# Conv loads begun under the stage before them: shared pools, weights by planes, first images of the last stage in memory early

## The chip, the core and the metric

The kernel runs on one core of a Trainium2 chip. The metric is device microseconds for one execution. The kernel before takes 2425.87 us, the median of 3 runs (2424.24 to 2426.80). The profile is of one further execution, which took 2423.68 us; its recorded span is 2421.5 us.

## What is computed

The input x has 8 images of 256 channels and 56 x 56 pixels, in float32. Two layers follow each other, both of the form "x plus f(group norm of x)".

```python
def _L0_conv_ref(x, w_reduce, b_reduce, w_span, b_span):
    ker = einsum('bchw,oc->bohw', x, w_reduce) + b_reduce
    ker = einsum('bchw,oc->bohw', ker, w_span) + b_span
    ker = ker.reshape(B, G, 1, K * K, H, W)
    ...
    out = (ker * patches).sum(axis=3)

def _L1_conv_ref(x, w1, w2, g1, b1, g2, b2):
    out1 = noised_tri_conv(x, w1)
    out1 = batch_norm_train(out1, g1, b1)
    out1 = jax.nn.relu(out1)
    out2 = noised_tri_conv(out1, w2)
    out2 = batch_norm_train(out2, g2, b2)
    return jax.nn.relu(out1 + out2)

x = x + _L0_conv_ref(_gn(x), ...)
x = x + _L1_conv_ref(_gn(x), ...)
```

The first layer is an involution: each pixel has its own 7 x 7 filter for each of 16 groups. The second layer has two 3 x 3 convolutions with weights quantized to -1, 0 and 1 (the centre tap counts twice). Batch norm needs the mean and variance of a whole convolution's output before the next step may start, so the layer is cut into stages that can't be merged.

## The kernel before, in words

There are four stages, and what one leaves for the next lies in DRAM: x1 (after the involution), y1 (after convolution 1), y2 (after convolution 2).

**Involution** (lines 435 to 864). The 8 images are worked in 32 quarters of 64 channels. Inside a quarter, ten rows of tiles follow each other. For each row TensorE multiplies the filter matrices `a` with input tiles `q` (`apply_row`, L704), ScalarE and VectorE pick the result out of PSUM (L716, L717), and GpSimd adds it to x (L720). Filters of the next quarter are made meanwhile (L671, L675, L680). A hand-written order is pinned on every engine. At the end of a quarter x1 is stored (L732), and after the last quarter one call of `group_norm_params` (L858) makes the scale and shift of the second group norm for all 8 images.

**Convolutions** (`conv_phase`, L242, called once for each). A pass n takes half an image (28 output rows); there are 16 passes. It loads two `raw` tiles (L264), normalizes them on ScalarE into the padded tile `xp` (L870 in convolution 1, L880 with ReLU in convolution 2), and VectorE makes six row-transformed planes of them (`transform`). Each plane is kept as a high part (ScalarE, L294) and a low part (VectorE, L295), whose sum is the float32 value. TensorE then does 6 planes x 2 output halves x 12 matmuls = 144 matmuls of 128 x 392 (L388), in the order of `ORDER`. VectorE combines the planes to rows of y (L374 and L399 to L410), SyncE stores y (L420), and ScalarE sums y and its square for the batch norm (`statistics`, L351), one pass late. The weights are one tile of 4608 KB, loaded at the stage's start (L249). Every pool of the stage is opened at its start and given back at its end.

**Batch norm parameters** (`batch_norm_params`, L163) are a chain of small instructions, mostly on VectorE.

**Last stage** (L887 to L900). For 16 half-channel images it loads y1, y2 and x1 (1568 KB each), does ReLU, multiply-add, ReLU and an add, and stores the result. y1 and y2 have two buffers each, x1 three.

Loads and stores from SyncE go through one queue in program order: an instruction that waits holds up all behind it. The order on each engine is made when the program is built, by a scheduler with priorities.

Of the kernel before, what the change touches and what calls it, by code (L numbers as in the profile page):

```python
# [13 lines left out]
DRAM = bass.MemoryType.DRAM  # L14

P = 128
# [62 lines left out]
def involution_tri_block_kernel(  # L79
# [33 lines left out]
    st1, st2 = (const_tile([P, CT, 2, 2 * B], name) for name in ("st1", "st2"))  # L113
# [128 lines left out]
    def conv_phase(stack, i, src_d, norm, stats, shift, dst_d):  # L242
# [4 lines left out]
        wqp = stack.enter_context(tc.tile_pool(name=f"wq{i}p", bufs=1))  # L247
        wq = wqp.tile([P, WT, CT, 3, C], F32R, tag="wq", name=f"wq_{i}")
        nc.sync.dma_start(wq.rearrange("p w t k o -> p (w t k o)").bitcast(F32), wq_d[i - 1])  # L249
        pad = stack.enter_context(tc.tile_pool(name=f"pad{i}", bufs=1))  # L250
        planes = stack.enter_context(tc.tile_pool(name=f"planes{i}", bufs=8))
        wk = stack.enter_context(tc.tile_pool(name=f"wk{i}", bufs=1))
        ps_c = stack.enter_context(tc.tile_pool(name=f"ps_c{i}", bufs=4, space=PSUM))

        xp = pad.tile([P, 4, CT, HT + 1, WP], F32, tag="xp", name=f"xp_{i}")
        nc.gpsimd.memset(xp, 0.0)

        def load(n):
            b, h = n // 2, n % 2
            raws = []  # L260
            for t in range(CT):
                raw = wk.tile([P, RAW * W], F32, tag=f"raw{t}", name=f"raw{i}_{n}_{t}")
                r0 = h * (H - RAW)
                nc.sync.dma_start(raw, src_d[b][t][:, r0 * W:(r0 + RAW) * W])  # L264
                raws.append(raw)
            return raws

        def temp(name, tag, bufs):
            return wk.tile([P, CT, HT * WP], F32, tag=tag, bufs=bufs, name=name)

        def transform(n, raws, out):

            b, h = n // 2, n % 2
            edge = xp[:, 0, :, 0, :] if h == 0 else xp[:, 1, :, HT, :]
            nc.gpsimd.memset(edge, 0.0)  # L275
            for f in (2, 0, 1, 3):
                r0 = (f - 1) % 4 if h == 0 else f
                m_ = len(range(r0, RAW, 4))
                i0 = (r0 + 1 - h) // 4
                for t in range(CT):  # L280
                    norm(xp[:, f, t, i0:i0 + m_, 1:1 + W],
                         raws[t].rearrange("p (h w) -> p h w", w=W)[:, r0::4, :], b, t)

            def d(k):
                return xp[:, k % 4, :, k // 4:k // 4 + HT, :].rearrange("p t r w -> p t (r w)")

            def lin(dst, x, c, y):

                nc.vector.scalar_tensor_tensor(dst, x, c, y, ALU.mult, ALU.add)  # L289

            def keep(k, r):
                hi, lo = (planes.tile([P, CT, HT * WP], F32R, tag=f"pl{j}",
                                      name=f"pl{i}_{n}_{k}_{j}") for j in range(2))
                nc.scalar.copy(hi, r)  # L294
                nc.vector.tensor_tensor(lo, r, hi.bitcast(F32), ALU.subtract)  # L295
                out[k] = [v.rearrange("p t (r w) -> p t r w", w=WP) for v in (hi, lo)]

            def tmp(name):
                return temp(f"{name}{i}_{n}", "ta", 4)

            def res(k):
                return temp(f"r{k}{i}_{n}", "tr", 4)

            p, q = tmp("p"), tmp("q")
            lin(p, d(2), -4.0, d(4))
            lin(q, d(1), -4.0, d(3))
            yield
            r = res(1)
            nc.vector.tensor_tensor(r, p, q, ALU.add)
            keep(1, r)  # L310
            r = res(2)
            nc.vector.tensor_tensor(r, p, q, ALU.subtract)
            keep(2, r)
            yield
            u, v = tmp("u"), tmp("v")
            nc.vector.tensor_tensor(u, d(4), d(2), ALU.subtract)
            nc.vector.tensor_tensor(v, d(3), d(1), ALU.subtract)
            yield
            r = res(3)
            lin(r, u, 0.5, v)  # L320
            keep(3, r)
            r = res(4)
            nc.vector.scalar_tensor_tensor(r, u, 0.5, v, ALU.mult, ALU.subtract)
            keep(4, r)
            yield
            a = tmp("a")
            lin(a, d(0), 4.0, d(4))
            r = res(0)
            lin(r, d(2), -5.0, a)
            keep(0, r)  # L330
            yield
            a = tmp("a5")
            lin(a, d(1), 4.0, d(5))
            r = res(5)
            lin(r, d(3), -5.0, a)
            keep(5, r)
            yield

        def statistics(n, y):
# [8 lines left out]
            for to in range(CT):  # L348
                for j, f in enumerate((AF.Identity, AF.Square)):
                    dummy = wk.tile([P, NH], F32, tag="dummy", name=f"dummy{i}_{n}_{to}_{j}")  # L350
                    nc.scalar.activation(dummy, y[:, to], f, bias=shift[:, to:to + 1],  # L351
                                         accum_out=stats[:, to, j, n:n + 1])
                    yield

        done = iter(())
        nxt = {}
        raws = load(0)
        for _ in transform(0, raws, nxt):
            pass
        raws = load(1)  # L360
        for n in range(2 * B):
# [4 lines left out]
            next(steps, None)  # L366
            if n + 2 < 2 * B:
                raws = load(n + 2)
# [12 lines left out]
            for k in ORDER:  # L381
                ps = ps_c.tile([P, CT, 512], F32, tag="conv", name=f"c{i}_{n}_{k}")
                for to in range(CT):
                    c, last = 0, CT * 3 * 2 - 1
                    for t in range(CT):
                        for dx in range(3):
                            for part in cur[k]:
                                nc.tensor.matmul(  # L388
                                    ps[:, to, :NM], wq[:, k, t, dx, to * P:(to + 1) * P],
                                    part[:, t, :, dx:dx + W], start=(c == 0), stop=(c == last))  # L390
                                c += 1
                m[k] = ps[:, :, :NM].rearrange("p o (r w) -> p o r w", w=W)
# [8 lines left out]
                elif k == 4:  # L401
# [6 lines left out]
                    for z, z2, c in ((s, s2, 0.5), (d, d2, 4.0)):  # L408
                        flat, flat2 = (v.rearrange("p o r w -> p (o r w)") for v in (z, z2))
                        nc.vector.scalar_tensor_tensor(flat, flat2, c, flat,  # L410
                                                       ALU.mult, ALU.subtract)
                elif k == 0:
                    row_of(0, m[0], 1.5, s, ALU.add)
                elif k == 5:
                    row_of(3, m[5], 6.0, d, ALU.add)
                next(steps, None)
# [5 lines left out]

        for _ in done:
            pass
# [10 lines left out]
    with ExitStack() as ph1:  # L435
# [9 lines left out]
        xpool = ph1.enter_context(tc.tile_pool(name="xpool", bufs=2 * NCQ - 1))  # L445
        fix = ph1.enter_context(tc.tile_pool(name="fix", bufs=1))
        work = ph1.enter_context(tc.tile_pool(name="work", bufs=2))
# [39 lines left out]

        gst1, mvs = {}, {}
# [5 lines left out]
        def fixed(shape, name, src=None):  # L494
            t_ = fix.tile(shape, F32, tag=name, name=name)
# [3 lines left out]

        ident_sb = fixed([P, P], "ident_sb", ident)  # L500
        half_sb = fixed([P, 2], "half_sb", half)
        wr, wrn = fixed([P, NCQ, CR], "wr"), fixed([P, NCQ, 2 * CR], "wrn")
# [4 lines left out]
        wl = fixed([P, NCQ, GP, WL], "wl", w_line)  # L507
        bt = fixed([NQ, NCQ, GQ, NP], "bt", b_tile)
        kr = [fixed([P, PX, NT + (NE if py == 0 else 0)], f"kr{py}") for py in range(PY)]

        side_sb = fixed([P, 2], "side_sb", side)

        xn = fixed([P, NK, SR, QX], "xn")
# [266 lines left out]
        apool = ph1.enter_context(tc.tile_pool(name="apool", bufs=1))  # L780
# [30 lines left out]
        for m, (b, c) in enumerate(quarters):  # L811
# [7 lines left out]
            for ty in range(TY):  # L819
# [13 lines left out]
                if more and r >= 20:  # L833
                    if r == 20:
                        norm = params(b + 1)
# [22 lines left out]
        for _ in group_norm_params(mv2.rearrange("p b t s -> p (b t) s"),  # L858
                                   gn2h.rearrange("p b t s -> p (b t) s"), ps_flat, "gn2"):
            pass  # L860

        for h in range(2):
            rows = slice(h * CH, (h + 1) * CH)
            nc.vector.tensor_copy(gn2[rows], gn2h[rows, :, h::2, :])
# [3 lines left out]
    with ExitStack() as ph2:  # L868
        def norm_x1(dst, src, b, t):
            nc.scalar.activation(dst, src, AF.Identity,  # L870
                                 bias=gn2[:, b, t, 1:2], scale=gn2[:, b, t, 0:1])

        conv_phase(ph2, 1, x1_d, norm_x1, st1, nc1, y1_d)
# [3 lines left out]
    sc1, bi1 = batch_norm_params(st1, nc1, g1_sb, b1_sb, "bn1")  # L877
    with ExitStack() as ph3:
        def norm_y1(dst, src, b, t):
            nc.scalar.activation(dst, src, AF.Relu, bias=bi1[:, t:t + 1], scale=sc1[:, t:t + 1])  # L880

        conv_phase(ph3, 2, y1_d, norm_y1, st2, nc2, y2_d)
# [4 lines left out]
    with tc.tile_pool(name="fin", bufs=2) as fin:  # L887
        for b in range(B):
            for t in range(CT):
                y1 = fin.tile([P, HW], F32, tag="y1", name=f"y1f_{b}_{t}")  # L890
                nc.sync.dma_start(y1, y1_d[b][t])
                y2 = fin.tile([P, HW], F32, tag="y2", name=f"y2f_{b}_{t}")
                nc.sync.dma_start(y2, y2_d[b][t])
                x1 = fin.tile([P, HW], F32, tag="x1", bufs=3, name=f"x1f_{b}_{t}")
                nc.sync.dma_start(x1, x1_d[b][t])
# [73 lines left out]
```

## Time and profile before

| what | value |
|---|---|
| median of 3 runs | 2425.87 us |
| profiled execution | 2423.68 us |
| its span | 2421.5 us |
| TensorE busy | 1885.9 us (78%) |
| VectorE busy | 1671.0 us (69%) |
| ScalarE busy | 1261.0 us (52%) |
| GpSimd busy | 592.9 us (24%) |
| mean TensorE clock granted | 0.896 |

Times in the profile are microseconds from the start of the span. PE is TensorE's matmuls, PEld its weight loads, DVE VectorE, ACT ScalarE, POOL GpSimd, SP SyncE. A view by windows gives, for stretches that one chooses, busy time and number of instructions of each engine, the granted TensorE clock (1.00 is full), the mean busy share of the 16 DMA engines and what they moved. The stages are, by their first and last instructions: involution to 1256.7, convolution 1 from 1278.8 to 1707.4, convolution 2 from 1739.2 to 2168.4, last stage to 2421.5.

### The profile page before, as it was taken

To read this page: it belongs to the slowest core of one execution; us is meant where nothing else is said; L and a number is where in the kernel's file an instruction comes from. 1 tells how busy PE (TensorE), PEld (TensorE's weight loads), DVE (VectorE), ACT (ScalarE), POOL (GpSimd) and SP (SyncE) were. 2 spreads that over 40 slices of the span, in tenths; PEclk is the share of its full clock that TensorE was granted. 3 is DMA by queue.
4 is the path that set the end of the run, shared out by engine and by line. 5 is a ranking of instruction groups with operands and counts; after the bars stand their busy time and mean duration, and the time that the engine had idled before them with its cause. 6 is when DMAs were issued, how large, how long until landed. Compare 5 with 4: busy or idle time off the path is not lost.

```text
span 2421.5 us, 72092 instructions
## 1 busy us (share of the span) xinstructions
PE 1885.9 (78%) x31080; PEld 1711.2 (71%) x31080; DVE 1671.0 (69%) x2570; ACT 1261.0 (52%) x2404; POOL 592.9 (24%) x1325
## 2 busy tenths in 40 slices
PE   3419898989899898989968999999499999980000
PEld 2217777777777777777858999999499999980000
DVE  6277465564746466574649999999599999974444
ACT  1105454545545454555645667666466677653333
POOL 2404463545546364554630000000000000000000
PEclk8559999999999999999988999999799999995555
DMA  4426363654636364553553233222432233229998
GB/s 155 152 99 177 106 198 109 182 151 144 187 110 206 90 198 137 160 173 107 161 185 149 109 132 137 112 109 106 176 123 109 109 136 136 109 111 430 430 430 377
DMA packets 124441, 406.46 MB, mean 168 GB/s; under 512 B 25694, under 2 KB 32220, under 8 KB 115420
## 3 DMA queue, kind: packets, MB, share of 16 engines
q1 hardware_dynamic: 117664, 360.89, 43.5%
q10 hardware_dynamic: 6460, 40.97, 4.2%
q8 instruction: 244, 4.00, 0.7%
q14 instruction: 73, 0.60, 0.1%
HBM read 259.33 MB, written 142.48 MB: 166 GB/s over the span
## 4 chain that ended last, share of the span: by engine, by line
PE 41%; DMA 10%; DVE 2%; ACT 1%; issue 1%; SPq 0%; POOL 0%; ACTq 0%; DVEq 0%
PE c L388 35%; DMA y1f<-y1d 3%; PE pg L671 3%; DMA out_y<-x1f 2%; DMA x1f<-x1d 2%; PE pa L704 2%; DVE x1f L899 1%; PE ptq L638 1%; DMA y2f<-y2d 1%; DMA y1d<-y 1%; DMA wq<-wqd 1%; PE pk L538 0%; PE pt L605 0%; ACT a L675 0%; DVE a L680 0%
## 5 line engine op out<-in xcount | busy, mean ns | idle before, releaser
L388 PE MATMUL c<-pl,wq 128*128 128x392 f32 x4608 | 857.3, 348 | 51.3 <-ACT pl L294 32.0
L388 PEld LDWEIGHTS c<-pl,wq 128*128 128x128 f32 x4608 | 855.4, 189 | 53.1 <-ACT pl L294 32.8
L680 DVE TENSOR_TENSOR a<-pg,bt 126x756 f32<-126x756 f32 (+3 forms) x640 | 393.8, 656 | 283.2 <-ACT a L675 225.7
L671 PE MATMUL pg<-kr,wl 64*126 64x140 f32 (+1 forms) x6144 | 460.9, 293 | 56.8 <-DVE a L680 32.5
L671 PEld LDWEIGHTS pg<-kr,wl 64*126 64x126 f32 x6144 | 394.8, 194 | 112.0 <-issue 70.3
L704 PE MATMUL pa<-a,q 126*32 126x48 f32 x17920 | 270.4, 208 | 71.5 <-DMA q<-xtd 44.5
L641 ACT COPY q<-ptq 126x384 f32<-126x384 f32 x320 | 153.0, 478 | 314.0 <-issue 171.0
L675 ACT ACTIVATE a<-pg,bt 126x126 f32<-126x126 f32 x768 | 242.5, 475 | 136.0 <-PE pg L671 136.0
L704 PEld LDWEIGHTS pa<-a,q 126*32 126x32 f32 x17920 | 221.7, 111 | 128.5 <-issue 89.4
L720 POOL TENSOR_TENSOR x<-x,inv 128x168 f32<-128x168 f32 x320 | 165.5, 517 | 577.4 <-DVE inv L717 557.0
L717 DVE SCALAR_TENSOR_TENSOR inv<-pa,half_sb,inv 128x168 f32<-128x168 f32 x320 | 118.6, 371 | 213.3 <-ACT inv L716 212.2
L294 ACT CAST pl<-r 128x812 fp32r<-128x812 f32 x192 | 162.4, 867 | 153.0 <-DVE r L289 136.4
L351 ACT ACTIVATE dummy<-y,nc 128x1568 f32<-128x1568 f32 x128 | 205.3, 1604 | 15.6 <-DVE y L374 14.3
L295 DVE TENSOR_TENSOR pl<-r,pl 128x812 fp32r<-128x812 f32 x192 | 186.3, 996 | 30.6 <-ACT pl L294 29.7
L275 POOL MEMSET xp<- 128x116 f32 x32 | 6.3, 196 | 817.7 <-DVE a L289 817.6
L561 POOL TENSOR_SCALAR xn<-x,gn 128x224 f32<-128x224 f32 (+2 forms) x384 | 184.2, 500 | 29.1 <-PE pt L605 18.5
L638 PE MATMUL ptq<-ident_sb,xe 128*126 128x128 f32 x960 | 178.6, 296 | 9.4 <-ACT stg L608 7.0
L561 POOL TENSOR_SCALAR xe<-x,gn 128x168 f32<-128x168 f32 (+2 forms) x384 | 160.3, 437 | 19.9 <-DVE gn L161 19.9
L139 DVE BATCH_NORM_STATS2 st<-x 128x6 f32<-128x392 f32 x256 | 138.0, 555 | 9.9 <-DMA x<-in_x 9.3
L608 ACT COPY stg<-pt 98x512 f32<-98x512 f32 x128 | 79.9, 624 | 122.0 <-PE pt L605 61.6
L716 ACT ACTIVATE inv<-pa,half_sb 128x168 f32<-128x168 f32 x320 | 126.9, 397 | 1.9 <-PE pa L704 1.8
L638 PEld LDWEIGHTS ptq<-ident_sb,xe 128*126 128x126 f32 x960 | 101.3, 143 | 29.7 <-ACT stg L608 7.2
(134 smaller groups left out, 1740.2 us busy)
## 6 DMA issues: line engine op xcount, KB each, us to landing
q<-xtd SPq DMA_DIRECT2D x320, 252.0 KB
raw<-x1d SPq DMA_DIRECT2D x32, 812.0 KB
raw<-y1d SPq DMA_DIRECT2D x32, 812.0 KB
x<-in_x SPq DMA_DIRECT2D x64, 392.0 KB
xtd<-stg SPq DMA_DIRECT2D x128, 196.0 KB
x1d<-x SPq DMA_DIRECT2D x64, 392.0 KB
y1d<-y SPq DMA_DIRECT2D x32, 784.0 KB
y2d<-y SPq DMA_DIRECT2D x32, 784.0 KB
```

The lines of the kernel that those rows point to most:

```text
L294: nc.scalar.copy(hi, r)
L295: nc.vector.tensor_tensor(lo, r, hi.bitcast(F32), ALU.subtract)
L351: nc.scalar.activation(dummy, y[:, to], f, bias=shift[:, to:to + 1], accum_out=stats[:, to, j, n:n + 1])
L388: nc.tensor.matmul(ps[:, to, :NM], wq[:, k, t, dx, to * P:(to + 1) * P], part[:, t, :, dx:dx + W], start=(c == 0), stop=(c == last))
L561: nc.gpsimd.tensor_scalar(dst[:, i - d - k0:f - d - k0, :, x0:x0 + n], v[:, i:f, :, j0:j0 + n], scale, bias, ALU.mult, ALU.add)
L638: nc.tensor.transpose(pt[:NQ, k * P:(k + 1) * P], xe[c % 2][:, k, PY * ty:PY * ty + QY].rearrange("p r x -> p (r x)"), ident_sb)
L641: nc.scalar.copy(loads[b, c, ty][:NQ, NK:].rearrange("p k c -> p (k c)"), pt[:NQ, :NX * P])
L671: nc.tensor.matmul(dst, wl[rows, c, gp, o:o + NQ], kr[py][rows, px, :], start=True, stop=True)
L675: nc.scalar.activation(whole[:, g0 + i, p0 + j], ps[:NQ, i, j * nt:(j + 1) * nt], AF.Identity, bias=bt[:, c, g0 + i, p0 + j:p0 + j + 1])
L680: nc.vector.tensor_tensor(dst[:, g0:g0 + 2, p0:p0 + nv].rearrange("q g p t -> q g t p"), ps[:NQ, :, t0 * nv:t1 * nv].rearrange("q i (t p) ...
L704: nc.tensor.matmul(ps[o:o + 32, k * 2 * n:(k + 1) * 2 * n], q[:NQ, k, o:o + 32], av[:, t + k, g * 2 * n:(g + 1) * 2 * n], start=True, stop ...
L720: nc.gpsimd.tensor_tensor(xv, xv, iv.rearrange("p t (y x) -> p y t x", x=PX), ALU.add)
```

## The change

1. **Memory.** The pools of the convolutions (`rawp`, `wqp`, `pad`, `tmpp`, `planes`, `wk`, `ps_c`) are opened once for both. In the involution `apool` (the filter matrices of even quarters), and a new pool `early` (`kr`, `wl`, `bt`) are opened first, and the images' pool goes to the other end of memory (`side="right"`). So the raw tiles and the weights of convolution 1 lie where `apool` lay, and `xp` where `early` lay.
2. **Convolution 1's start.** The scale and shift of the second group norm are made for images 0 to 6 in the last image's rows, and for image 7 at the end. The first `raw` tiles and `xp` can be begun in the last quarter.
3. **Weights by planes.** Six tiles of 768 KB take the place of one of 4608 KB. In the last pass of convolution 1 each plane's weights for convolution 2 are loaded as soon as that plane's matmuls are done. The first `raw` tiles of convolution 2 are loaded in the pass before.
4. **Matmul order.** Inside a group of 12 matmuls the high part's six come first, then the low part's six; before, the two parts alternated on the same weights.
5. **First transform.** At n == 0 the second channel half is normalized on VectorE instead of ScalarE.
6. **Statistics of the last pass.** They are summed in three portions (rows 1 and 2, row 0, row 3 of each four) as the rows are made, into two more columns of the statistics.
7. **Last stage.** The buffers come from three pools `fa`, `fb`, `fc`, laid over memory that convolution 2 gives back at different times.

```diff
-    st1, st2 = (const_tile([P, CT, 2, 2 * B], name) for name in ("st1", "st2"))
+    st1, st2 = (const_tile([P, CT, 2, 2 * B + 2], name) for name in ("st1", "st2"))
...
+    def weights(i, k):
+        w = wqp.tile([P, CT, 3, C], F32R, tag=f"wq{k}", name=f"wq{i}_{k}")
+        n = CT * 3 * C
+        nc.sync.dma_start(w.rearrange("p t k o -> p (t k o)").bitcast(F32),
+                          wq_d[i - 1][:, k * n:(k + 1) * n])
+        return w
...
                     norm(xp[:, f, t, i0:i0 + m_, 1:1 + W],
-                         raws[t].rearrange("p (h w) -> p h w", w=W)[:, r0::4, :], b, t)
+                         raws[t].rearrange("p (h w) -> p h w", w=W)[:, r0::4, :], b, t,
+                         nc.vector if n == 0 and t else nc.scalar)
...
+        def last_rows(n, y, k0, m):
+            for _ in sums(n, [y[:, to].rearrange("p (r k) -> p r k", k=4 * W)
+                              [:, :, k0 * W:(k0 + m) * W] for to in range(CT)]):
+                pass
...
-        raws = load(1)
+        raws = load(i, 1, src_d)
...
+            final = n == 2 * B - 1
             if n + 2 < 2 * B:
-                raws = load(n + 2)
+                raws = load(i, n + 2, src_d)
+            elif not final and follow:
+                begun = {}, load(i + 1, 0, dst_d)
...
-                    for t in range(CT):
-                        for dx in range(3):
-                            for part in cur[k]:
+                    for part in cur[k]:
+                        for t in range(CT):
+                            for dx in range(3):
                                 nc.tensor.matmul(
-                                    ps[:, to, :NM], wq[:, k, t, dx, to * P:(to + 1) * P],
+                                    ps[:, to, :NM], wq[k][:, t, dx, to * P:(to + 1) * P],
...
+                if final and follow:
+                    begun[0][k] = weights(i + 1, k)
...
+                    if final:
+                        last_rows(n, y, 1, 2)
                 elif k == 0:
                     row_of(0, m[0], 1.5, s, ALU.add)
+                    if final:
+                        last_rows(n + 1, y, 0, 1)
                 elif k == 5:
                     row_of(3, m[5], 6.0, d, ALU.add)
+                    if final:
+                        last_rows(n + 2, y, 3, 1)
...
-        xpool = ph1.enter_context(tc.tile_pool(name="xpool", bufs=2 * NCQ - 1))
+        apool = ph1.enter_context(tc.tile_pool(name="apool", bufs=1))
+        early = ph1.enter_context(tc.tile_pool(name="early", bufs=1))
         fix = ph1.enter_context(tc.tile_pool(name="fix", bufs=1))
+        xpool = ph1.enter_context(tc.tile_pool(name="xpool", bufs=2 * NCQ - 1, side="right"))
...
-                if more and r >= 20:
+                if r >= 20:
                     if r == 20:
-                        norm = params(b + 1)
+                        norm = params(b + 1) if more else gn2_params(0, b)
...
+        begun = load(1, 0, x1_d)
+        begun = {k: weights(1, k) for k in ORDER}, begun
+        xp = pad.tile([P, 4, CT, HT + 1, WP], F32, tag="xp", name="xp")
+        nc.gpsimd.memset(xp, 0.0)
+        begun = conv_phase(1, begun, x1_d, norm_x1, st1, nc1, y1_d, True)
...
+                nc.vector.tensor_scalar(dst, src, scale, bias, ALU.mult, ALU.add)
+                nc.vector.tensor_scalar(dst, dst, 0.0, None, ALU.max)
...
-    with tc.tile_pool(name="fin", bufs=2) as fin:
+        fa, fb, fc = (ph4.enter_context(tc.tile_pool(name=name, bufs=1))
+                      for name in ("fa", "fb", "fc"))
+        homes = {"y1": (fc, fa), "y2": (fc, fb), "x1": (fc, fb, fb)}
+        def loaded_image(name, j, src):
+            k = j % len(homes[name])
+            v = homes[name][k].tile([P, HW], F32, tag=f"{name}{k}", name=f"{name}f_{j}")
+            nc.sync.dma_start(v, src)
+            return v
```

In the built program the involution's instructions keep their order, engine by engine, up to its last two quarters. In them these are put in: on SyncE's queue the first `raw` tile between the `q` loads of rows 3 and 4 of the last quarter, and the second `raw` tile and the first plane of weights behind the last `q` load, ahead of the last two x1 stores; the other five planes follow those stores. On ScalarE four normalizations between rows 1 and 4 of the last quarter. On GpSimd the clearing of `xp` ahead of the add of the quarter before's last row. In the last pass of convolution 2, the queue of SyncE has y1 of the second and y1 and y2 of the first image of the last stage ahead of the last two y2 stores, and x1 of the first and all else behind them.

## The prediction

> **What bounds the kernel now.** I read the 40 slices first, then busy time by windows that I set on the places where TensorE pauses, then the chain of waits in order of time.
>
> ```profile
> PE   3419898989899898989968999999499999980000
> ...
> PEclk8559999999999999999988999999799999995555
> DMA  4426363654636364553553233222432233229998
> ```
>
> Each digit is a tenth of a 60 us slice. PE stands at 9 through both convolutions, but falls to 6 and 4 at the two borders before them and to 0 in the last stage, where DMA goes to 9.
>
> ```profile
> 1256.00:1279.00 23.00, 1.52 (x5) 1.23 (x6) 10.64 (x25) 7.02 (x11) 4.11 (x4) 0.52 0.90 344
> 1708.00:1741.00 33.00, 1.42 (x3) 0.60 (x3) 9.25 (x23) 13.75 (x19) 0.00 (x0) 0.54 0.79 292
> 1741.00:1955.00 214.00, 214.00 (x1149) 213.88 (x1150) 205.47 (x250) 139.94 (x188) 1.57 (x8) 0.99 0.31 116
> 2169.00:2200.00 31.00, 0.00 (x0) 0.00 (x0) 13.08 (x18) 17.15 (x13) 0.00 (x0) 0.54 0.99 397
> 2200.00:2412.00 212.00, 0.00 (x0) 0.00 (x0) 96.73 (x28) 84.22 (x29) 0.00 (x0) 0.50 1.00 427
> ```
>
> Columns: length, busy PE, PEld, DVE, ACT, POOL with counts, clock, DMA share, GB/s. Inside a convolution PE is busy all the time and DVE 205 of 214. At the borders nothing but DMA is busy, and the last stage is DMA at 427 GB/s. So a border is worth what its transfers hold up, and the last stage what can be moved out of it.
>
> ```profile
> 1257.28 7.14 DMA x1d<-x
> 1264.55 14.12 DMA wq<-wqd
> 1278.81 428.52 PE c L388 x2304
> 1707.35 1.05 DVE y L374 x2
> 1708.41 17.27 DMA y1d<-y
> 1725.89 4.20 DMA raw<-y1d
> 1730.27 5.05 ACT xp L880 x8
> ...
> 1740.98 427.43 PE c L388 x2302
> 2168.43 1.05 DVE y L374 x2
> ```
>
> These rows are start, length, what. The chain runs through weights at the first border and through y1 stores and raw loads at the second.
>
> **Part by part.** Sums are against the profiled execution (2423.68 us, span 2421.5).
>
> *Border 1.* Before, PE starts convolution 1 at 1278.81; the last involution add ends at 1256.72. After, weights and raw tiles lie in memory free since quarter 30, so neither 7.14 nor 14.12 stays on the path. What is late next is the chain on DVE behind that add. Durations from DVE's rows: statistics 0.57, aggregate 0.26, four small ones 0.8 for image 7, three of the four normalizations, p, q, r1 at 0.92, 0.92, 1.00. A normalization is not in the trace on DVE; tensor_scalar rows of 128x128 (0.287) and 128x1536 (1.086) give 0.44 for 392 elements, bounded by 0.29 and 0.56 (the 392-element scalar_tensor_tensor). Sum 5.9, plus 0.5 for the matmul wait and 0.9 for the ACT cast: 7.3. Five planes (768 KB each) queue behind the x1 stores, 1.8 us each at 430 GB/s; PE eats one in 4.5 us, so they are covered; uncovered, each costs 1.8.
>
> This has a price. The first raw tile goes on SP's queue ahead of the `q` load of row 4; behind it wait six `q` loads and through them PE. It moves 831 KB; `raw<-y1d` took 4.20 for two, so it lands some 2.5 to 4 us after its issue near 1240. ACT's first normalization stands behind the pick-out of row 1 (1241.3) and waits for it, with `q` copies of rows 4 to 9 queued behind, then adds four of 0.71 = 2.8. ACT has about 0.5 us a row idle there. POOL's clearing (3.19) sits ahead of one add. Bounds: nothing, and 5; I take 2.5, the ACT wait. Some fourteen small DVE instructions (0.2 each) for images 0 to 6 lie under filter making. Last, DVE's built order in the first pass of convolution 1 puts s, d and s2 (which wait for PE planes 2 and 4) ahead of the next pass's p; laid out at 0.92 us a step, the row that frees plane 3's PSUM bank comes some 2.7 us late. Bounds 0 and 3.5; I take 1.5. PE after: 1256.7 + 2.5 + 7.3 = 1266.5. **Gain 12.3 - 1.5 = 10.8.**
>
> *Border 2.* Before: last row at 1708.40, four sums of 1568 elements (1.73 apart) to 1714.9, parameters 2.8 to 1717.7, then nothing until raw tiles land at 1730.1, since their loads stood behind the 4.6 MB of weights and the y stores. After, raw tiles are there a pass earlier. The sums become twelve: from 1568 elements in 1.604 and 3136 in 2.999 a piece of 784 takes 0.91, one of 392 0.56, each plus 0.13. Rows 1 and 2 are ready at 1702.5, so ACT runs 4 x 1.04 + 8 x 0.69 = 9.7 to 1712.1: it gains 2.8, not the whole tail, because ACT is now the late one. Parameters to 1714.95. DVE then normalizes its half in eight instructions (multiply-add, maximum) of 0.44: 3.5, then p, q, u, r1 and the cast, 4.7: PE at 1723.2, where it was 1739.19, and the second weights' wait (PE continuous only from 1740.98, two matmuls in between) goes: another 1.1. Weights are covered by 16 us. **Gain 17.** Bounds: 13 (DVE at 0.56, raw late by a queue) and 20.
>
> *Last stage.* Its bound is bytes. Three loads of 1568 KB get ahead of the last pass; x1 of the first image and all of the second stand behind the last y2 stores, which wait for the last row. So 4.82 MB at 430 GB/s leave the stage: 11.2 us. Given back: ACT now has the 3.00 us ReLU of image 0 between its sums, so the parameters end no more than 2 us sooner, and y1 of image 2 waits for the first add; I estimate 1 us of DMA idle more. **Gain 10.** Bounds 6 and 13.
>
> *At nothing:* the involution up to its last quarters, same order, same waits; second clearing of `xp`, on an idle POOL; two more statistics columns.
>
> **The matmul order** meets a rule. The Trainium skill, TensorE: Matmul & The Clock Gate, Part 2, step 1, says that loading and computing are split so that weights are loaded once and multiplied repeatedly; before, high and low shared their weights back to back, after they don't.
>
> ```profile
> L388 PE MATMUL c<-pl,wq 128*128 128x392 f32 x4608 | 857.3, 348 | 51.3 <-ACT pl L294 32.0
> L388 PEld LDWEIGHTS c<-pl,wq 128*128 128x128 f32 x4608 | 855.4, 189 | 53.1 <-ACT pl L294 32.8
> ```
>
> There are as many loads as matmuls, so nothing was shared; start to start from 1400 to 1480 odd and even steps take 184 and 185 ns, so a repeated load is no cheaper. By the row the edit costs 0; by the rule, at the page's 107 ns for a 128-column load (estimate), 2304 lost sharings unhidden would cost 246. I take 0.
>
> **The clock** is the second. The same page (Part 1) has PE at half clock after an idle window of 3.4 us.
>
> ```profile
> 1278.80:1280.80 2.00, 2.00 (x6) 0.50 1.02 426
> 1280.80:1282.80 2.00, 2.00 (x7) 0.50 0.20 81
> 1282.80:1284.80 2.00, 2.00 (x9) 0.65 0.00 0
> ```
>
> 22 matmuls in the first 6 us instead of 33 at 0.182: 2.0 us a border. By the rule's window gaps of 11 and 16 us still start cold, so I credit none of it; if the border were called closed, it would be 4 more.
>
> **Sum:** 10.8 + 17 + 10 = 38: 2423.7 - 38 = 2385.7 for the profiled execution. That lay 2.2 under the median shown, so 2388 for a median.
>
> **Rivals.**
> - *Less: the waits are only exchanged.* The last quarter pays 5 and the first pass 3.5 (border 1: 5), border 2 gives 13, the stage 6: -24, 2402. For: ACT and SP are in order, and DVE has 9 of 214 us spare. Against: the involution's last quarter makes no filters, so engines are light. 0.18.
> - *More:* the raw tile lands before ACT asks and DVE's order does no harm (border 1: 15), 20 and 13: -48, 2378. For: PE waited on `q` and code there anyway. Against: DMA is at 0.9 to 1.09 at 1242 to 1246. 0.14.
> - *No change:* the loads are not early after all. The built waits name only long-finished work for them; against it speaks all of border 2. 0.02.
> - *Slower: matmul pace.* If the part order costs each of 4608 matmuls over 38/4608 = 8.2 ns (185 to 193), the sum turns; at 107 ns on half of them it would be 2388 + 246 = 2634. Against: the equal steps above. 0.03.
>
> **Numbers.** Forecast 2388, chance 0.63, own range 2380 to 2396; with both neighbours 2376 to 2402 holds 8 in 10. A measurement of this kernel tells 0.2% (4.9 us) from no change. Faster 0.95, same 0.02, slower 0.03.
>
> **What would show it.** Border 1: first convolution matmul some 10 us after the last add, ACT waiting for `raw<-x1d` in the last quarter, its end about 2.5 later. Border 2: ACT sums to about 5 us after the last matmul, no DMA wait. Last stage: y1 and two others landed before the last matmul, span after it near 243 us where it was 253. PE inside the convolutions: 148 matmuls in 27 us as before. I am wrong if that pace moves, if the chain still names weights or raw loads, or if DMA in the last stage drops under 9 tenths.

## The result, and the profile after

| kernel | median, us | kernel before, run beside it | ratio |
|---|---|---|---|
| changed, first measurement | 2397.32 (2392.70 to 2398.49) | 2425.05 | 0.9883, 95% interval 0.9866 to 0.9900 |
| changed, once more (`a0_again`) | 2386.89 (2385.92 to 2395.35) | 2418.86 | 0.9877, 0.9853 to 0.9901 |

The change makes the kernel 1.2% faster: 28 and 32 us in the two measurements, where the sum forecast 38 (2388 us, own range 2380 to 2396, with both neighbours 2376 to 2402). The profiled execution took 2392.7 us with a span of 2390.8, 30.7 less than the span before.

The page of the changed kernel, by slices of 60 us (a digit is the busy share of its slice, in tenths):

```profile
PE   3419898989889898998988999999799999980000
...
PEclk8559999999999999999998999999899999995555
DMA  4425364654636365463554422332532233249998
```

At the first border TensorE's lowest digit was 6 (slice 21) and is 8 (slice 22); at the second it was 4 and is 7 (slice 29). The last stage is DMA at 9 as before. Both convolutions still start at half clock. Their first 2 us (length, busy PE with count, clock, DMA share, GB/s):

```profile
1268.87:1270.87 2.00, 2.00 (x6) 0.50 0.97 353
1716.42:1718.42 2.00, 2.00 (x6) 0.50 0.31 119
```

The view by windows of the changed kernel (length, busy PE, PEld, DVE, ACT, POOL with counts, clock, DMA share, GB/s), set on the chain from the last add to convolution 1, its first pass, the border between the convolutions, eight passes of convolution 2, and four parts of the last stage:

```profile
1262.40:1268.90 6.50, 1.22 (x5) 1.04 (x5) 6.16 (x15) 0.96 (x3) 0.00 (x0) 0.50 0.82 210
1268.90:1296.00 27.10, 27.10 (x137) 26.99 (x138) 21.78 (x32) 11.56 (x17) 0.20 (x1) 0.92 0.65 248
1700.10:1716.40 16.30, 0.33 (x2) 0.00 (x0) 10.80 (x30) 9.28 (x22) 0.00 (x0) 0.60 0.69 235
1716.40:1930.40 214.00, 213.99 (x1147) 213.64 (x1148) 206.65 (x251) 140.63 (x189) 1.57 (x8) 0.99 0.31 117
2145.00:2165.00 20.00, 0.00 (x0) 0.00 (x0) 9.22 (x18) 10.87 (x23) 0.00 (x0) 0.55 0.95 386
2165.00:2168.00 3.00, 0.00 (x0) 0.00 (x0) 3.00 (x2) 0.00 (x0) 0.00 (x0) 0.50 0.74 222
2197.00:2200.00 3.00, 0.00 (x0) 0.00 (x0) 3.00 (x2) 0.92 (x1) 0.00 (x0) 0.50 0.72 205
2205.00:2380.00 175.00, 0.00 (x0) 0.00 (x0) 79.49 (x23) 70.49 (x24) 0.00 (x0) 0.50 1.01 428
```

At the first border VectorE now works 6.16 of 6.5 us; before, it worked 10.64 of 23 there and the chain of waits ran through DMA. In 214 us of convolution 2 TensorE does 1147 matmuls, before 1149: the pace stands. Two lines are new: in the first pass of convolution 1 VectorE is busy for only 21.8 of 27.1 us, and in the last stage DMA drops to 0.74 and 0.72 in two holes.

The chain of waits of the changed kernel (start, length, what):

```profile
1261.42 0.96 POOL x L764 x2
1262.41 0.57 DVE st L141
1262.98 0.41 DVE xp L918
...
1266.87 0.97 DVE r L314
1267.94 0.88 ACT pl L299
1268.87 37.69 PE c L409 x192
1306.67 0.43 issue
1307.34 1.32 ACT xp L916 x2
...
1335.98 355.56 PE c L409 x1920
...
1705.24 0.72 ACT dummy L364 x2
1708.87 0.93 DVE xp L936 x2
...
1716.41 428.38 PE c L409 x2304
2144.82 1.05 DVE y L395 x2
```

Weights and raw loads are gone from both borders; statistics, normalization and one cast have taken their place, as forecast. But the chain leaves TensorE in convolution 1 at 1306.67 and stays with it again only from 1335.98. In between it runs through ScalarE's normalization and VectorE, and TensorE pauses three times, 2.3 us in all:

```profile
1307.50 13.62 PE L409 MATMUL c<-pl,wq 128*128 128x392 f32 x72 [0.96 <-ACT e L419]
1322.29 13.52 PE L409 MATMUL c<-pl,wq 128*128 128x392 f32 x72 [1.18 <-DVE d L423]
1335.98 9.30 PE L409 MATMUL c<-pl,wq 128*128 128x392 f32 x49 [0.17 <-DVE y L395]
```

**The account by stages.** The runs are compared by marks in the trace: duration of a quarter from its rows on VectorE, start of first and last matmuls of a convolution. Each run has one trace; the five without a ratio below (`b3`, `b4`, `c1`, `c2`, `c4`) were executed once, so only their stages are read. The involution has 320 rows. Row 300 ends anywhere from 1210.9 to 1221.7 us in twelve traces whose involution is the same up to there, so whole times scatter by some us and single stages are what tells. Quarter 30 took 29.1 to 30.3 us in the nine traces that share its code with the changed kernel; its rows 21 to 24, in which the new parameters fall, took 13.9 in each of them.

| step | forecast gain | profiled execution | `a0_again` |
|---|---|---|---|
| quarter 30 (26.5 before) | 0 | -2.6 | -2.7 |
| quarter 31 (18.0 before) | -2.5 | -3.3 | -2.7 |
| last add to first matmul (22.1 before) | 14.8 | 15.6 | 15.6 |
| convolution 1, first to last matmul (428.2 before) | -1.5 | -3.1 | -3.6 |
| last matmul to convolution 2 (32.2 before) | 16.0 | 15.9 | 15.9 |
| convolution 2 (428.9 before) | 1.1 | 0.8 | 0.6 |
| last stage (253.5 before) | 10 | 7.1 | 7.0 |
| sum | 38 | 30.4 | 30.1 |

### The profile page after: what moved, and what is told of

Same layout as the page of the kernel before. It is cut to its first block, busy times and chain, and to the rows that moved or that the text cites. A ratio compares the mean times of both kernels' runs of the same rounds, so it can differ in the third digit from the quotient of the medians.

```text
span 2390.8 us, 72175 instructions
## 1 busy us (share of the span) xinstructions
PE 1889.8 (79%) x31084; PEld 1712.6 (72%) x31084; DVE 1675.6 (70%) x2596; ACT 1261.1 (53%) x2429; POOL 590.2 (25%) x1324
## 5 line engine op out<-in xcount | busy, mean ns | idle before, releaser
L409 PE MATMUL c<-pl,wq 128*128 128x392 f32 x4608 | 857.6, 348 | 20.6 <-ACT pl L299 18.3
L364 ACT ACTIVATE dummy<-y,nc 128x1568 f32<-128x1568 f32 (+2 forms) x144 | 210.1, 1459 | 5.3 <-DVE y L429 3.5
L605 POOL TENSOR_SCALAR xn<-x,gn 128x224 f32<-128x224 f32 (+2 forms) x384 | 184.7, 501 | 27.1 <-PE pt L649 18.5
L141 DVE BATCH_NORM_STATS2 st<-x 128x6 f32<-128x392 f32 x256 | 138.0, 555 | 10.6 <-DMA x<-in_x 9.4
L682 PEld LDWEIGHTS ptq<-ident_sb,xe 128*126 128x126 f32 x960 | 101.2, 143 | 29.2 <-ACT stg L652 6.7
```

What stands on the lines that cost most here:

```text
L364: nc.scalar.activation(dst, v, f, bias=shift[:, to:to + 1], accum_out=stats[:, to, j, n:n + 1])
L409: nc.tensor.matmul(ps[:, to, :NM], wq[k][:, t, dx, to * P:(to + 1) * P], part[:, t, :, dx:dx + W], start=(c == 0), stop=(c == last))
L605: nc.gpsimd.tensor_scalar(dst[:, i - d - k0:f - d - k0, :, x0:x0 + n], v[:, i:f, :, j0:j0 + n], scale, bias, ALU.mult, ALU.add)
L682: nc.tensor.transpose(pt[:NQ, k * P:(k + 1) * P], xe[c % 2][:, k, PY * ty:PY * ty + QY].rearrange("p r x -> p (r x)"), ident_sb)
```

## Experiments

**The changed kernel again.**

> The changed kernel once more, nothing edited, for its spread and for a second trace. Of the 38 us of the sum some 31 arrived in its profiled execution and 28 in its median. If the missing part is built in, the second trace shows it at the same four places: quarter 30 of the involution near 29.1 us (26.5 before the change), the end of the involution near 1262, convolution 1 some 3 us longer than before, last stage after the last matmul near 246.5. If it is drift of that one execution, these move by 2 us or more. Median 2393 to 2399.

Quarter 30 took 29.2 us, the last add came at 1264.25 (row 300 was 2.4 later), convolution 1 took 431.75, the last stage 246.47. The missing part is built in, at four places; the table holds it.

**Quarter 30: small instructions in a shared ring.** The parameters of the second group norm for images 0 to 6 are made in rows 20 to 22 of the last image.

```diff
-                gn2h[...], ps_flat, f"gn2_{b0}")
+                gn2h[...], ps_spare, f"gn2_{b0}")
+        def ps_spare(name):
+            return ps_a.tile([P, 512], F32, tag="pt", name=name)
```

> Scale and shift of the second group norm for images 0 to 6 take their PSUM tiles from the ring of the transposes instead of the ring in which filters are made. Theory A (each of the two tiles held one of the two filter buffers for a row, so filter making stood): rows 21 and 22 of the last image go from 4.9 and 4.4 back towards 3.1 and 1.7, quarter 30 from 29.1 to about 26.5, all later marks 2.7 us earlier. Theory B (the small instructions themselves, or TensorE waiting for VectorE's second small step, cost it): quarter 30 stays within 0.7 of 29.1.

Quarter 30 fell to 27.8: half of A. Row 21 went from 4.9 to 3.6, row 22 stayed at 4.4. So the ring is half of it. TensorE's wait for VectorE's `d` ahead of the second small matmul is a second part; `b1` below tries it. Both are seen in TensorE's timeline, first before the change, then in the changed kernel:

```profile
1212.68 1.70 PE L671 MATMUL pg<-kr,wl 64*126 64x140 f32 x24
```

```profile
1212.41 0.33 PE L148 MATMUL gnp_gn<-mv,grp_sb 128*128 128x56 f32 x2
1212.66 0.98 PE L715 MATMUL pg<-kr,wl 64*126 64x140 f32 x12
1215.01 0.98 PE L715 MATMUL pg<-kr,wl 64*126 64x140 f32 x12 [1.36 <-DVE a L724]
...
1217.90 0.38 PE L157 MATMUL gnp_gn<-d_gn,grp_sb 128*128 128x28 f32 x2 [0.70 <-DVE d_gn L155]
```

Filter matmuls (`pg`) that ran as one group of 24 before are cut in two: the small result `gnp_gn` sits in one of their two PSUM tiles until VectorE copies it, a row later.

**The last pause of the involution.** First try:

```diff
+        stored = nc.cur_bb.bb.instructions[-1]
         begun = {k: weights(1, k) for k in ORDER}, begun
+        behind(nc.cur_bb.bb.instructions[-6])
```

> The first plane of weights for convolution 1 is queued behind the last two x1 stores instead of ahead of them. Theory A (the last code fetch of TensorE waits behind 1580 KB of raw tile and weights in the DMA engines): with 768 KB less ahead, the pause before the last 80 odd matmuls of the involution shrinks from 3.9 us to about 2.1 and the last add comes 1.8 earlier relative to row 7 of the last quarter; with it convolution 1 starts 1.8 earlier. Theory B (the pause is the fetch's own time under any load): it stays at 3.5 to 4.3. The built order of convolution 1's first passes on ScalarE also changes in this kernel, so its first passes are not compared.

The pause before the last matmuls was still there in part (1.97 us, and one of 2.0 a few rows sooner), quarter 31 took 20.6 and the fetch began no earlier (table below). The built order had put plane 2 into the place of plane 1, so 1580 KB were still ahead: the run says nothing on the theory. Convolution 1 took 428.45 us in it, 3 less, with another order of ScalarE in its first passes; but its first matmul came 8.56 us after the last add instead of 6.49, so some 1 us of that is gain. A second try ordered all weights and the raw tiles of pass 1 behind the stores; another, everything.

```diff
+        for i in nc.cur_bb.bb.instructions[-6:]:
+            behind(i)
+        if i == 1:
+            for v in nc.cur_bb.bb.instructions[-2:]:
+                behind(v)
```

> Of the loads of convolution 1 only the two raw tiles stay ahead of the last x1 stores; all weights and the raw tiles of pass 1 are queued behind them. (The earlier run meant to test this left the bytes ahead as they were, since plane 2 took plane 1's place in the queue.) Theory A (the last code fetch of the involution stands behind the loads that were issued just before it): with 812 KB instead of 1580 KB ahead, the fetch starts 1.5 to 2 us sooner, near 15 us after row 9 of the quarter before instead of 16.6, the pause of 3.6 to 3.9 us before the last matmuls shrinks to about 2, and quarter 31 falls from 21 to about 19. Theory B (the fetch is late for another reason): pause and quarter stay. The weights now come after the last add, so convolution 1's start is not compared.

> All loads of convolution 1, raw tiles and weights, queued behind the last two x1 stores, with ScalarE's four normalizations behind the involution; the clearing of xp on GpSimd stays where it was. Theory A (the 3 us of the last quarter are the loads, the code fetch behind them and ScalarE's wait): quarter 31 falls from 21 to about 18, as before the change; the first matmul then comes some 10 to 13 us after the last add instead of 6.5, since raw tiles and weights are late. Theory B (GpSimd's clearing and the changed state of the queues cost it): quarter 31 stays near 20 to 21.

From the DMA records of the instruction queue; the start of TensorE's last fetch in quarter 31, in us after row 9 of quarter 30, and the length of TensorE's pauses "issue" of over 1 us up to its last matmuls there. The last pause ends 1.3 us after the fetch in the first, second and fifth line. (The queue is taken for TensorE's, since before the change it carries 4.00 of 4.60 MB of fetches and TensorE has 62160 of 72092 instructions.)

```
kernel               KB ahead   fetch starts   last pause   pause before   quarter 31
before                     0       14.0           1.4          1.9            18.0
changed                 1580       16.75          3.9          none           21.3
a0_again                1580       16.5           3.6          none           20.7
a2_plane_behind         1580       16.5           2.0          2.0            20.6
c1_one_load_ahead        812       14.7           2.0          1.3            18.8
b4_loads_behind            0       13.6           none         1.0, 2.2       18.4
```

c1 decides for A in all three numbers. Rows 30 to 37 take 15.7 us in the changed kernel and in c1, and the last two 5.6 and 3.1 (before: 15.5 and 2.5). Up to its first matmul c1 gains next to nothing by this, since that comes 8.90 us after the last add instead of 6.49. The end of the involution in the chain before the change, and then the changed kernel and c1 in TensorE's timeline:

```profile
1252.50 0.55 PE pa L704 x32
1253.05 1.38 issue
```

```profile
1255.14 0.53 PE L748 MATMUL pa<-a,q 126*32 126x48 f32 x28
1259.57 1.57 PE L748 MATMUL pa<-a,q 126*32 126x48 f32 x84 [3.89 <-issue]
```

```profile
1261.15 0.53 PE L751 MATMUL pa<-a,q 126*32 126x48 f32 x28
1263.65 1.01 PE L751 MATMUL pa<-a,q 126*32 126x48 f32 x84 [1.97 <-issue]
```

The pause is named "issue", that is, nothing that the profile shows as a wait; the fetch of 16 KB of TensorE's instructions is what was found to end just before, and to move with it. In b4 the fetch before it, from 9.1, is the one that stops TensorE (2.2 us). The wait that I had charged, ScalarE's for the raw tile, is there too, one line in the changed kernel's timeline:

```profile
1246.39 0.72 ACT L916 ACTIVATE xp<-raw,gn 128x392 f32<-128x392 f32 x1 [2.62 <-DMA raw<-x1d]
```

It delays rows 31 and 32 by 1.9 us together, but before the change row 34 took 3.6 us, with a fetch of its own, and now takes 1.9: that wait is paid back. b4 also prices the early loads: its first matmul came 17.07 us after the last add (I had expected 10 to 13; ScalarE's normalizations are then behind the raw tiles too) instead of 6.49. They bring 10.6 and cost 2.9 in quarter 31. Convolution 1 took 427.38 us in b4, so 3.9 more of their gain was lost there; the next run asks where.

**The first passes of convolution 1.**

```diff
-        begun = {k: weights(1, k) for k in ORDER}, begun
+        begun = {k: weights(1, k) for k in ORDER[:2]}, begun
...
         raws = load(i, 1, src_d)
+        for k in ORDER:
+            if k not in wq:
+                wq[k] = weights(i, k)
```

> The raw tiles of pass 1 of convolution 1 are queued ahead of four of the six planes of weights; the built order then has the next pass's transform ahead of s and d of pass 0 on VectorE. Theory A (VectorE stood at s and d of pass 0 and had no spare time to catch up): the 3.1 us that TensorE lost in passes 1 and 2 go to under 1, so that convolution 1 takes about 428.5 to 429 us from its first to its last matmul instead of 431.5. Theory B (weights or raw tiles arrive too late in either order): TensorE still loses 2 to 3, or stands at plane 3, whose weights now wait for the second raw tile's buffer.

Convolution 1 took 427.54 us, and passes 0 and 1 28.1 and 26.7 instead of 28.6 and 29.3. The other four planes of weights, now queued behind the raw tiles, were in time. VectorE in the first pass, in the view by windows of this run:

```profile
1268.20:1295.30 27.10, 27.10 (x139) 26.96 (x140) 27.07 (x38) 14.34 (x20) 0.20 (x1) 0.94 0.63 248
```

27.07 of 27.10 us instead of 21.78. In the changed kernel it had stood twice, both times at `s`:

```profile
1280.80 0.98 DVE L422 TENSOR_TENSOR s<-c,e 128x784 f32<-128x784 f32 x1 [1.05 <-ACT e L419]
1289.71 0.97 DVE L427 TENSOR_TENSOR s<-c,e 128x784 f32<-128x784 f32 x1 [4.17 <-ACT e L419]
```

These 5.2 us are missing when passes 1 and 2 need them. But the edit moves two things. By the DMA records the raw tiles of pass 1 landed at 1279.6 and 1282.6 in the changed kernel and at 1271.2 and 1273.7 here, and ScalarE's first normalization of them began at 1284.4 and 1273.1. So the changed order of the loads is the cause, but whether it works through late raw tiles or through VectorE's order alone was not separated.

**Three mends together.**

```diff
+        fa, fb, fc, fd = ...
+        homes = {"y1": (fc, fa, fd), "y2": (fc, fb, fd), "x1": (fc, fb, fb, fd)}
...
         nc.vector.tensor_tensor(d, d, d, ALU.mult)
+        if name.startswith("gn2"):
+            yield
```

(with the two edits above, the ring and the raw tiles)

> Three edits in three stages, each read at its own marks. (1) The parameters of the second group norm for images 0 to 6 use the spare PSUM ring and have one row more between VectorE's d and the second small matmul. Theory A (half of the 2.7 us was the ring, the other half TensorE waiting in row 22 for VectorE's d): quarter 30 falls to 26.5 to 27; theory B (the instructions themselves): it stays at 27.8 as with the ring alone. (2) Raw tiles of pass 1 ahead of four planes of weights, as before: convolution 1 takes 427.5 to 428.5. (3) A third buffer each for y1 and y2 and a fourth for x1 in the last stage. Theory A (the DMA engines stand 2.4 us because loads wait for buffers that the late parameters keep): the time after the last matmul falls from 246.4 to about 244.5, and the holes near 22, 33 and 54 us after the last matmul go. Theory B (the stage is bound by bytes and by slower mixed reads and writes): it stays within 0.5 of 246.4. All of A: 8 to 9 us below the changed kernel, if a like drift of the involution is taken.

Quarter 30: 27.2, and 27.5 in `b2` below with the same edit; before the change it was 26.5. Row 22 falls from 4.4 to 1.2, but row 23 takes 5.7 instead of 1.7. Rows 21 to 24 together took 10.7 us before the change, 13.9 after, 12.6 with the ring alone, 12.0 here and 12.3 in `b2`. So the ring is worth 1.3 and the row between 0.3 to 0.6; the cause of the remaining 1.3 to 1.5 stays open. Convolution 1: 427.79. Last stage: 242.30, twice A's gain. Its windows at the places of the two holes:

```profile
2164.00:2167.00 3.00, 0.00 (x0) 0.00 (x0) 3.00 (x2) 0.00 (x0) 0.00 (x0) 0.50 0.99 406
2196.00:2199.00 3.00, 0.00 (x0) 0.00 (x0) 2.33 (x1) 0.00 (x0) 0.00 (x0) 0.50 0.99 422
```

By the DMA records the stage moves 104.4 MB before the change, 99.6 after and in this run. The 16 DMA engines stand 6.9, 9.2 and 7.0 us on average, and while they work they move 423, 420 and 423 GB/s. With enough buffers the whole 11.2 us of the 4.8 MB arrive (253.5 - 242.3). The median was 2383.75, ratio 0.9833 (0.9816 to 0.9849).

**The last stage's pool and ScalarE alone; sums at the end.**

```diff
-        homes = {"y1": (fc, fa), "y2": (fc, fb), "x1": (fc, fb, fb)}
+        homes = {"y1": (fin,) * 2, "y2": (fin,) * 2, "x1": (fin,) * 3}
...
-                         nc.vector if n == 0 and t else nc.scalar)
+                         nc.scalar)
```

> Two edits in two stages. (1) The last stage's buffers come from one pool with the counts of before (2, 2, 3), so that of its loads one instead of three lies ahead of the last pass's y2 stores. My account (three loads are worth 11.2 us, of which 4.1 were given back as idle and mixed DMA time): with 3.2 MB more after the last matmul and less given back, 250 to 252 us instead of 246.4. (2) The first transform of a convolution is normalized on ScalarE alone. My step (VectorE takes half): the 16.3 us between the convolutions become 17.8 to 18.5; rival (ScalarE's eight normalizations are as fast as VectorE's sixteen instructions): under 0.7 more.

The last stage took 252.30 us, 5.9 more; from convolution to convolution 17.64, 1.3 more. Both lie just outside the intervals I gave, on the side named. At the first border ScalarE alone was no slower: 6.25 us from the last add to the first matmul instead of 6.49.

```diff
-                    if final:
-                        last_rows(n, y, 1, 2)
...
+        for _ in done:
+            pass
         return begun
```

> The statistics of the last pass are summed at its end, as before the change, instead of in three portions. My step (the portions end ScalarE's sums 2.8 us sooner): 16.3 us from the last matmul of convolution 1 to the first of convolution 2 become about 19, and the last stage about 2 us longer than 246.4. Rival (the raw tiles or the normalization end the wait anyway): under 1 us at both places.

18.36 from convolution to convolution (2.0 more, not 2.8) and 247.73 in the last stage (1.3 more).

**The matmul order.**

```diff
-                    for part in cur[k]:
-                        for t in range(CT):
-                            for dx in range(3):
+                    for t in range(CT):
+                        for dx in range(3):
+                            for part in cur[k]:
```

> The matmul order of before (high and low part alternate on the same weights), all else as in the changed kernel. My step (the order costs nothing): 148 matmuls in 27 us in either, the middle passes of convolution 1 26.6 us each. The rule's reading (a repeated load is cheaper when weights are used twice in a row): passes shorter by up to 0.5 us or more each.

Middle passes take 26.60 us in the old order and 26.65 in the new one: 0.3 ns a matmul, 0.7 us over a convolution. But the first pass of convolution 2 takes 29.96 in the old order (29.88 before the change) and 28.43 in the new: TensorE can begin with six high matmuls while VectorE still makes the low part. In the old order the second and third matmul wait:

```profile
1723.87 0.69 PE L409 MATMUL c<-pl,wq 128*128 128x392 f32 x1 [16.03 <-ACT pl L299]
1724.79 0.69 PE L409 MATMUL c<-pl,wq 128*128 128x392 f32 x1 [0.23 <-ACT pl L299]
1725.71 24.58 PE L409 MATMUL c<-pl,wq 128*128 128x392 f32 x122 [0.23 <-DVE pl L300]
```

Net, the order brings 0.6 to 0.8 us in convolution 2 (428.84 against 428.03 and 428.27), and it is where the 0.8 and 0.6 us of the table come from; I had put down 1.1 there to the second weights' wait.

**What the same wait costs elsewhere.** In images 0 to 6, rows 21 to 23 make the first group norm's parameters of the next image in the same way.

```diff
-            yield from group_norm_params(mvs.pop(b), dst, ps_flat, f"a{b}")
-            ps = ps_flat(f"br_{b}")
+            yield from group_norm_params(mvs.pop(b), dst, ps_spare, f"a{b}")
+            yield
+            ps = ps_spare(f"br_{b}")
...
-        STRIPS_AT = 23
+        STRIPS_AT = 24
```

(and the `yield` in `group_norm_params` for every image)

> As the run with three mends, and the parameters of the first group norm of the next image, made in rows 20 to 23 of images 0 to 6, get the same treatment: PSUM tiles from the ring of the transposes and a row between each step. In the trace of before, rows 21 to 23 of these images take 4.8, 4.7 and 8.0 us, of the last image 3.1, 1.7 and 3.4. Theory A (the same two waits): 3 to 6 us less an image, 20 to 40 us in all, and faster than both kernels. Theory B (these rows are long because of other work, the next image's transposes and loads): under 1 us an image.

> The kernel before the change, with only the spare PSUM ring and the extra rows for the first group norm's parameters of images 0 to 6. Theory A (the 10 us an image that run b2 gained have nothing to do with the change): quarter 2 of each image falls from 50 to about 40, row 300 comes near 1130, median near 2425 - 75 = 2350; against it the changed kernel with the same edits (2310) keeps its gain of 35 to 40. Theory B (the gain needs the change's memory): under 20.

| rows of images 0 to 6, mean us | row 21 | row 22 | row 23 | quarter with them |
|---|---|---|---|---|
| before | 5.0 | 4.6 | 8.2 | 48.8 to 50.3 |
| c3 (before, mended) | 3.5 | 1.3 | 4.9 | 39.8 to 42.3 |
| b2 (changed, mended) | 3.5 | 1.3 | 4.9 | 39.8 to 40.1 |

b2 is the fastest kernel here: median 2310.45 us, ratio 0.9525 (0.9503 to 0.9546). c3, without any part of the change, takes 2346.47, 0.9666 (0.9648 to 0.9683). The mend brings 80 us by itself in the medians (in c3's trace, the slowest of its five executions, row 300 comes 68 us sooner); the change and the two other mends bring another 34 to 36 (by the ratios, and 2346.47 - 2310.45). In b2's timeline of TensorE the group of filter matmuls is whole again:

```profile
1133.48 0.33 PE L148 MATMUL gnp_gn<-mv,grp_sb 128*128 128x56 f32 x2
...
1133.74 1.70 PE L723 MATMUL pg<-kr,wl 64*126 64x140 f32 x24
```

Which share of the 10 us an image is the ring, which the rows between the steps, and which the later start of the next image's preparation (`STRIPS_AT`), was not taken apart. The mean clock up to row 300 is also higher, 0.94 against 0.92.

## Why the prediction was right in sign and too high in size

- **Sign and mechanism right.** Both borders opened as the sum had it: 15.9 us between the convolutions against 16.0, and 6.5 us from the last add to the first matmul against 7.3. The reading that nothing but DMA was busy at the borders was wrong (VectorE worked 10.64 of 23 us at the first, ScalarE 13.75 of 33 at the second), but what held TensorE up there was DMA. The terms listed for the first border add up to 7.2, not 7.3, and a normalization on VectorE took 0.50 us, where 0.44 was estimated. The separate prices inside the second border were a little off: the early sums are worth 2.0 instead of 2.8, and VectorE's half of the normalization, not priced on its own, 1.3 there and nothing at the first border.
- **"At nothing" was wrong by 2.6.** The prediction counted the "fourteen small DVE instructions (0.2 each)" and let them lie under filter making. It did not count their two matmuls, which take one of the two PSUM tiles that filter making turns over, and one of which waits on VectorE. The run with the ring alone took back half of it (27.8), the ring and one row between together most of it (27.2 and 27.5); the rest is open.
- **The last quarter's 2.5 was the right size (3.0 as a mean) for a wrong reason, so it was luck.** The ScalarE wait named there exists and is paid back in row 34. What costs is the fetch of TensorE's instructions behind the loads issued a few us before it.
- **DVE's order in the first pass: 1.5 taken, 3.1 and 3.6 measured**, at and just past the upper bound of 3.5 (against a3, which is free of it, 3.7 and 4.2). I had laid out the lateness of one PSUM bank; the measured thing is 5.2 us in which VectorE stood at `s`, in a stage where it has 9 us in 214 to spare. The order that I had read was the built one, but that the raw tiles of pass 1 land behind six planes of weights was not in the sum.
- **Last stage: 10 taken, 7.1 measured.** The 11.2 us of bytes were right. The term "given back" was 1 and is 4.1: the DMA engines stand 2.3 us more, since loads in hand use up the buffers while the parameters are still being made, and move 0.8% less while they work. A third buffer for y1 and y2 and a fourth for x1 removes all of it.
- **Matmul order at 0 by the row against up to 246 us by the rule** (435 with the 189 ns that the trace's own load rows show): the row was right. What neither told is the gain in a cold first pass. It made up the 0.8 and 0.6 that arrived of the 1.1 credited to the second weights' wait; that this term came out near was luck too, since the two pauses behind it (0.16 and 0.23 us) were for ScalarE's high and VectorE's low part.
- **Clock.** TensorE still starts both convolutions cold, at 0.50, as the sum assumed.

Of the signs of being wrong that I named, two showed for a short while: the matmul pace in passes 1 and 2 (144 in 28 us from 1308, before 153), and the DMA share under 9 tenths in the two holes. They mark the two terms that were too good. The stage sum of 30 lies between my 38 and the 24 of the rival "less" (its terms for border 1 leave 6.3, not 5, so 25): its terms for the first pass (3.5) and the last stage (6) were nearer than mine, those for the last quarter (5) and border 2 (13) were not. Nothing of "no change" or of "matmul pace" was seen.

## What to carry to other kernels

A load that is moved under an earlier stage is not free just because its data path is idle: look at which instruction fetches and small loads will queue behind it, and at what stands behind its consumer in every in-order queue. A small instruction that is put into a busy loop must be priced by the buffer it borrows and the engine pair it ties together, not by its own 0.2 us; if the loop does the same elsewhere, measure that place first, since here it was worth more than twice the change. When loads are moved ahead of a stage bound by bytes, its buffers must grow with them, or the time comes back as holes.

## What was not expected of the hardware

- A fetch of 16 KB of instructions shares the DMA engines with data: it began at 16.75 us after row 9 with 1580 KB issued ahead of it, at 14.7 with 812 and at 13.6 with none, and TensorE stood 3.9, 2.0 and 0 us at it. The profile calls that idle time "issue".
- Whether it costs depends on where the fetch falls: in b2, with the same loads issued ahead of it, it began at 12.9, just as they were being issued, and quarter 31 took 17.4 us, less than before the change.
- The involution, unchanged up to row 300, reached it between 1210.9 and 1221.7 us. It moves every later mark with it.
